# Cross-attention with two softmaxes per head: the first four query chunks, the K and V projections, the output matmuls and the V copies are put in another order

## The chip, the cores and the metric

The kernel runs on one core of one Trainium2 chip. The metric is the device time of one launch in microseconds (us), from the first to the last instruction and what lies around them; the median of three runs is compared. Of the core, six things matter: TensorE (PE in the profile), its weight load (PEld), VectorE (DVE), ScalarE (ACT), GpSimd (POOL) and the SyncE queue that issues every DMA (SP).

## The reference

A cross-attention layer with 20 heads of 32 channels: 2 batches of 2048 queries with 640 channels, and 154 context rows with 1024 channels for each batch. The context is split in two halves of 77 rows, each with its own K and V weights and its own softmax; the two results are added, projected, and added to the input.

```python
q = split_heads(x @ Wq.T)
k, v = split_heads(text @ Wk.T), split_heads(text @ Wv.T)            # rows 0..76
k_ip, v_ip = split_heads(ip @ Wk_ip.T), split_heads(ip @ Wv_ip.T)    # rows 77..153
out = merge_heads(attend(q, k, v)) + merge_heads(attend(q, k_ip, v_ip))
return out @ Wo.T + bo + x
# attend: softmax(q k^T / sqrt(32)) v, per head
```

Everything is float32, and so in the kernel.

## The kernel before

**Tiles.** Tokens are taken in 4 blocks `j` of 1024 (blocks 0 and 1 are batch 0, blocks 2 and 3 batch 1), each with two halves `h` of 512. The 640 channels are 5 chunks `c` of 128, that is of 4 heads. One pass of the main loop (line 323), called a step here, computes the attention of one chunk of one block: `m = 5 j + c`, 20 steps, and a 21st for what is left. A step goes through its 1024 queries in three groups `s` of 3, 3 and 2 tiles of 128 queries.

**What a step does.** `scores(m, s)` multiplies queries with keys on PE, four heads in four row strips of the array (line 190, 12 or 8 matmuls), and ACT copies the result from PSUM to `pb` (line 197). `maxima` finds the row maxima on DVE (204) and subtracts them on POOL (205); `exponential` is on ACT (211); `sums` adds the rows and takes the reciprocal on DVE (218, 220); `normalise` multiplies on POOL (225); `transpose` turns 32x32 squares on DVE (231) into `tT`. `attend(m - 1)`, one step later, multiplies with V in sixteen 32x32 tiles of the array (line 244, 80 matmuls), and ACT copies its result to `aT` (251). Beside that a step computes the queries of the step after it, two groups of 5 matmuls (`queries`, line 165, copied by ACT in 173).

**PSUM.** Scores and attention share one buffer of four banks (tag `sc`, one buffer). So a group of scores can start only when ACT has copied the group before, and `attend` likewise. The other four banks are the four buffers of tag `mm`: queries, K, V and output.

**K and V.** Steps 0 to 4 also project V of their own chunk (`project_v`, two groups of 8 matmuls, line 123, between the queries and `scores(m, 1)`) and K of the next chunk (`project_k`, two such groups before `attend`). ACT copies them (130, 135). V is turned on DVE (`square_v`, line 138) and then laid out four times over by 16 small DMAs (`spread_v`, line 147), for both batches at once. The 20 weight tiles pass through five slots in the not yet used `aT` of block 1; a new one is loaded when a projection has read its slot.

**Output.** `Out` v is one of 40 output tiles (a half of a block, 128 channels): 5 matmuls (line 275), then bias and input added on DVE (`store`, 286) and a DMA to memory (289). The input tile it adds (`res`) is fetched one output ahead (267). Step m works on outputs `2 (m - 5)` and the next: the first before `attend`, the second after it. So steps 0 to 4 have none, and 10 are left after step 19. In the first step of a block the last matmul of an output waits for the `attend` just ahead of it.

**Order.** The order of each engine's instructions is that of the program text (`manual_schedule`); the framework adds the semaphores. All DMAs go through SP in that order too, and SP waits at a DMA until its buffer is free. At the start SP issues: half the context, a weight tile, the other half, another weight tile, the first 128 columns of `Wq`, five pieces of x, the rest of the block's x, two weight tiles, the other columns of `Wq`, a weight tile. PE then projects K of chunk 0, computes the queries of step 0 and enters the loop.

Of the kernel before, what the change touches and what calls it, by code (L numbers as in the profile page):

```python
# [8 lines left out]
F32 = mybir.dt.float32  # L9
# [4 lines left out]
B, S, C, CC, LT = 2, 2048, 640, 1024, 154  # L14
H, D, TEXT = 20, 32, 77
# [4 lines left out]
def kernel(  # L20
# [23 lines left out]
    nc = tc.nc  # L44
    P = 128
    NC = C // P
    NCC = CC // P
    G = P // D
    TB = 512
    NH = 2  # L50
    BLK = NH * TB
    NT = BLK // P
    NBLK = B * S // BLK
# [3 lines left out]
    NK = (2 * L + D - 1) // D  # L57
    LP = NK * D
    SCALE = 1.0 / float(D) ** 0.5
    NM = NBLK * NC  # L60
    NV = NBLK * NH * NC
    LEAD = NC

    const = ctx.enter_context(tc.tile_pool(name="const", bufs=1))
    qpool = ctx.enter_context(tc.tile_pool(name="qpool", bufs=5))
    small = ctx.enter_context(tc.tile_pool(name="small", bufs=4))
    opool = ctx.enter_context(tc.tile_pool(name="opool", bufs=2))
    rpool = ctx.enter_context(tc.tile_pool(name="rpool", bufs=3))
    ps_s = ctx.enter_context(tc.tile_pool(name="ps_s", bufs=1, space=bass.MemoryType.PSUM))
    ps_m = ctx.enter_context(tc.tile_pool(name="ps_m", bufs=4, space=bass.MemoryType.PSUM))  # L70

    wq = const.tile([P, NC, C], F32, name="wq")
    bo_sb = const.tile([P, NC], F32, name="bo_sb")
    kT = const.tile([P, NC, B, 2, L], F32, name="kT")
    v4 = const.tile([P, NC, B, G, NK, D], F32, name="v4")
    xs = [const.tile([P, NC, BLK], F32, name=f"x_{n}") for n in range(2)]
    aTs = [const.tile([P, NC, BLK], F32, name=f"aT_{n}") for n in range(2)]
    tT = const.tile([P, NT, G, NK, D], F32, name="tT")
# [3 lines left out]
        nc.gpsimd.memset(t[:, :, :, 2 * L :], 0.0)  # L82

    vTs = [const.tile([P, B, LP], F32, name=f"vT_{n}") for n in range(2)]
    vSs = [const.tile([P, B, LP], F32, name=f"vS_{n}") for n in range(2)]
    for t in vTs:
        nc.gpsimd.memset(t[:, :, 2 * L :], 0.0)

# [8 lines left out]
    def block_of(m):  # L97

        j, c = divmod(m, NC)
        return j, c, j * BLK // S  # L100
# [7 lines left out]
    def load_w():  # L108
        n = len(loaded)
        if n < len(wlist):  # L110
            src, c = wlist[n]
            w = wslots[n % len(wslots)]
            nc.sync.dma_start(  # L113
                out=w, in_=src[:, ts(c, P)].rearrange("(k p) o -> p k o", p=P)
            )
            loaded.append(w)
# [12 lines left out]
    def project_k(c, t):  # L129
        nc.scalar.copy(kT[:, c, :, t, :], project_kv(4 * c + t, t, "pk"))  # L130

    def project_v(c):
        vT = vTs[c % 2]
        for t in range(2):
            nc.scalar.copy(vT[:, :, ds(t * L, L)], project_kv(4 * c + 2 + t, t, "pv"))

    def square_v(c):
        nc.vector.transpose(
            vSs[c % 2].rearrange("p b l -> p (b l)"),
            vTs[c % 2].rearrange("p b l -> p (b l)"),  # L140
        )

    def spread_v(c):

        for g in range(G):
            for r in range(G):
                nc.sync.dma_start(
                    out=v4[r * D : (r + 1) * D, c, :, g].rearrange("p b k d -> p b (k d)"),
                    in_=vSs[c % 2][g * D : (g + 1) * D],
                )  # L150


# [5 lines left out]

    qTs = {}

    def queries(m, h):
        j, c, _ = block_of(m)
        pq = ps_m.tile([P, TB], F32, tag="mm", name=f"pq_{m}_{h}")
        for k in range(NC):
            nc.tensor.matmul(  # L165
                pq,
                wq[:, k, ts(c, P)],
                xs[j % 2][:, k, ts(h, TB)],
                start=(k == 0),
                stop=(k == NC - 1),  # L170
            )
        qT = qpool.tile([P, TB], F32, tag="qT", name=f"qT_{m}_{h}")
        nc.scalar.copy(qT, pq)  # L173
        qTs[(m, h)] = qT


    def keys_of(s):
# [57 lines left out]

    def attend(m):

        j, c, b = block_of(m)
        pa = ps_s.tile([P, G, 512], F32, tag="sc", name=f"pa_{m}")
        for k in range(NK):  # L240
            for r in range(G):
                rows = slice(r * D, (r + 1) * D)
                for g in range(G):
                    nc.tensor.matmul(  # L244
                        pa[g * D : (g + 1) * D, r, : NT * D],
                        v4[rows, c, b, g, k, :],
                        tT[rows, :, g, k, :],
                        start=(k == 0),
                        stop=(k == NK - 1),
                    )  # L250
        nc.scalar.copy(  # L251
            aTs[j % 2][:, c, :].rearrange("p (n r s) -> p r n s", n=NT, r=G),
            pa[:, :, : NT * D].rearrange("p r (n s) -> p r n s", n=NT),
        )


    class Out:


        def __init__(self, v):  # L260
            self.v = v
            self.j, r = divmod(v, NH * NC)
            self.h, self.o = divmod(r, NC)
            self.tok = ds(self.j * BLK + self.h * TB, TB)

            self.res = rpool.tile([P, TB], F32, tag="res", name=f"res_{v}")
            nc.sync.dma_start(out=self.res, in_=xT[ts(self.o, P), self.tok])
            self.po = None
            self.k = 0

        def step(self, n):
            if self.po is None:
                self.po = ps_m.tile([P, TB], F32, tag="mm", name=f"po_{self.v}")
            for _ in range(n):
                nc.tensor.matmul(  # L275
                    self.po,
                    wo[:, self.k, ts(self.o, P)],
                    aTs[self.j % 2][:, self.k, ts(self.h, TB)],
                    start=(self.k == 0),
                    stop=(self.k == NC - 1),  # L280
                )
                self.k += 1

        def store(self):
            ot = opool.tile([P, TB], F32, tag="ot", name=f"ot_{self.v}")
# [2 lines left out]
            )  # L288
            nc.sync.dma_start(out=outT[ts(self.o, P), self.tok], in_=ot)

    outs = {}

    def out(v):

        for w in (v, v + 1):
            if 0 <= w < NV and w not in outs:
                outs[w] = Out(w)
        return outs.get(v)


    half = NCC // 2
    for k in (0, half):
        nc.sync.dma_start(  # L303
# [1 line left out]
            in_=ctxT[ds(k * P, half * P), :].rearrange("(k p) n -> p k n", p=P),  # L305
        )
        load_w()
    nc.sync.dma_start(out=wq[:, :, :P], in_=WqT[:, :P].rearrange("(k p) o -> p k o", p=P))
    for k in range(NC):
        nc.sync.dma_start(out=xs[0][:, k, :TB], in_=xT[ts(k, P), :TB])  # L310
    load_x(0, 1)
    load_w()
    load_w()
    nc.sync.dma_start(out=wq[:, :, P:], in_=WqT[:, P:].rearrange("(k p) o -> p k o", p=P))
    load_w()
    nc.sync.dma_start(out=bo_sb, in_=bo.rearrange("(c p) -> p c", p=P))
    for t in range(2):
        project_k(0, t)
    for h in range(NH):
        queries(0, h)  # L320

    late = None
    for m in range(NM + 1):
        j, c, _ = block_of(m)
        new = m < NM
        old = m >= 1
        kv = m < NC
        v = NH * (m - LEAD)
        if new:
            scores(m, 0)  # L330
        if old:
            normalise(m - 1, 2)
        if late:
            late.store()
            late = None
        if old:
            transpose(m - 1, 1)
            transpose(m - 1, 2)
        if new:
            maxima(m, 0)  # L340
        if new and m + 1 < NM:
            queries(m + 1, 0)
        if c == 2 and j + 1 < NBLK:
            for h in range(NH):
                load_x(j + 1, h)
        if kv:
            project_v(m)
        if m == NC - 1:
            nc.sync.dma_start(out=wo, in_=WoT.rearrange("(c p) o -> p c o", p=P))
        if new:  # L350
            scores(m, 1)
            maxima(m, 1)
            exponential(m, 0)
            sums(m, 0)
            normalise(m, 0)
        if kv:
            square_v(m)
            spread_v(m)
        if new and m + 1 < NM:
            queries(m + 1, 1)  # L360
        if new:
            scores(m, 2)
            maxima(m, 2)
            exponential(m, 1)
            sums(m, 1)
            normalise(m, 1)
        if m + 1 < NC:
            project_k(m + 1, 0)
        if m + 1 < NC:
            project_k(m + 1, 1)  # L370
        first = c == 0
        if v >= 0 and v < NV:
            if new:
                out(v).step(NC - 1 if first else NC)
                if not first:
                    out(v).store()
            else:
                for w in range(v, v + 3):
                    out(w).step(NC - 1)
        if old:  # L380
            attend(m - 1)
        if new:
            transpose(m, 0)
            exponential(m, 2)
            sums(m, 2)
        if v >= 0 and new:
            if first:
                out(v).step(1)
                out(v).store()
            out(v + 1).step(NC)  # L390
            late = out(v + 1)
    for w in range(NH * (NM - LEAD), NV):
        out(w).step(NC - out(w).k)
        out(w).store()


# [30 lines left out]
```

## Time and profile before

| | |
|---|---|
| three runs | 559.28, 560.77, 562.39 us (median 560.77) |
| the profiled execution | 561.68 us, of which the span of its instructions is 559.9 us |
| PE busy | 530.7 us, 95% of the span |
| DVE, POOL, ACT busy | 377.1, 351.5, 231.4 us |
| data moved | 50.57 MB, 90 GB/s in the mean |
| first matmul starts | 6.72 us |
| steps 0, 1, 2, 3, 4, 5 last | 22.3, 24.8, 24.8, 26.0, 23.5, 28.7 us |
| steps 6 to 9 last | 24.0 us each |
| from step 19's first scores to the last output matmul | 68.1 us |

A step's length is the time from its first matmul of `scores(m, 0)` to that of the next step. In the profile a line such as "L190 PE" is line 190 of the kernel before. A float32 matmul is recorded as two passes, so that 5 matmuls read "x10". The profile is of one execution; its views are the busy times, the groups of instructions, who waited for whom, the chain of work that ended last, the instructions in order of time, and the busy times of chosen windows with the clock that TensorE was granted.

### The profile page before, as it was taken

The numbers are of one execution on the slowest core, as the hardware profiler recorded it, in microseconds if no ns is written. First come the engines' busy times: TensorE is split into PE (matmuls) and PEld (weight loads), VectorE is DVE, ScalarE is ACT, GpSimd is POOL, SyncE is SP. The second block draws the span as 40 slices with busy tenths as digits, with TensorE's granted clock in tenths as the row PEclk, the third lists the DMA queues.
The fourth block names the chain that finished last, engine by engine and source line by source line (L and its number), as shares of the span: only waits on it lengthen the run. The fifth ranks groups of instructions, "written<-read, shape, count | busy, mean of one in ns | idle before, by whom it ended". The sixth has DMA issues, their size and how long they took to land.

```text
span 559.9 us, 12327 instructions
## 1 busy us (share of the span) xinstructions
PE 530.7 (95%) x5600; PEld 285.2 (51%) x5600; DVE 377.1 (67%) x285; ACT 231.4 (41%) x201; POOL 351.5 (63%) x129
## 2 busy tenths in 40 slices
PE   5899999989979999999999999999999999989997
PEld 5477666656534445454444544545445454444442
DVE  0138778665877878787777877778777787777211
ACT  1244555444543553535445354544525455351000
POOL 0047868584885858669594776959668695866000
PEclk9999999989989999999999999999999999989999
DMA  9943567523302162020101252111020211112252
GB/s 285 330 118 90 127 185 215 131 50 118 83 5 76 40 226 66 12 77 23 54 24 54 74 190 77 39 39 45 33 77 1 76 40 37 46 33 95 84 148 89
DMA packets 47765, 50.57 MB, mean 90 GB/s; under 512 B 3808, under 2 KB 31072, under 8 KB 47712
## 3 DMA queue, kind: packets, MB, share of 16 engines
q1 hardware_dynamic: 47712, 49.77, 30.1%
q8 instruction: 44, 0.72, 0.5%
q14 instruction: 9, 0.07, 0.0%
HBM read 36.00 MB, written 10.49 MB: 83 GB/s over the span
## 4 chain that ended last, share of the span: by engine, by line
PE 88%; DMA 3%; POOL 3%; ACT 3%; DVE 1%; issue 1%; SPq 1%
PE po L275 31%; PE pq L165 28%; PE pa L244 12%; PE sc L190 9%; PE pv L123 4%; DMA wq<-in_L_xattn_Wq_dram 3%; PE pk L123 3%; POOL pb L225 2%; ACT aT L251 1%; POOL pb L205 1%; ACT pb L197 1%; SPq L113 1%; DVE mx L204 1%; DVE tT L231 0%; SPq L303 0%
## 5 line engine op out<-in xcount | busy, mean ns | idle before, releaser
L205 POOL TENSOR_TENSOR pb<-pb,mx 128x1848 f32<-128x1848 f32 (+1 forms) x60 | 176.4, 2942 | 140.2 <-DVE mx L204 140.2
L225 POOL TENSOR_TENSOR pb<-pb,rden 128x1848 f32<-128x1848 f32 (+1 forms) x60 | 176.4, 2943 | 20.8 <-DVE rden L220 17.0
L275 PE MATMUL po<-aT,wo_ct 128*128 128x512 f32 x400 | 181.2, 604 | 4.5 <-ACT aT L251 4.5
L165 PE MATMUL pq<-x,wq 128*128 128x512 f32 x400 | 183.7, 607 | 1.4 <-DMA wq<-in_L_xattn_Wq_dram 1.4
L204 DVE TENSOR_REDUCE mx<-pb 128x24 f32<-128x1848 f32 (+1 forms) x60 | 109.8, 1833 | 75.2 <-ACT pb L197 75.2
L218 DVE TENSOR_REDUCE den<-pb 128x24 f32<-128x1848 f32 (+1 forms) x60 | 111.8, 1863 | 34.1 <-ACT pb L211 34.1
L231 DVE STREAM_TRANSPOSE tT<-pb 128x1920 f32<-128x1920 f32 (+1 forms) x60 | 115.2, 1939 | 21.6 <-PE pa L244 20.0
L275 PEld LDWEIGHTS po<-aT,wo_ct 128*128 128x128 f32 x400 | 73.9, 191 | 96.7 <-issue 89.7
L197 ACT COPY pb<-sc 128x1848 f32<-128x1848 f32 (+1 forms) x60 | 91.8, 1529 | 65.8 <-PE sc L190 64.4
L165 PEld LDWEIGHTS pq<-x,wq 128*128 128x128 f32 x400 | 73.3, 191 | 85.8 <-issue 83.6
L211 ACT ACTIVATE pb<-pb 128x1848 f32<-128x1848 f32 (+1 forms) x60 | 94.6, 1577 | 51.2 <-POOL pb L205 51.1
L244 PE MATMUL pa<-tT,v 32*32 32x256 f32 x3200 | 70.1, 392 | 4.3 <-ACT pb L197 3.3
L190 PEld LDWEIGHTS sc<-kT,qT 32*128 32x128 f32 x1280 | 45.1, 185 | 48.3 <-issue 37.2
L190 PE MATMUL sc<-kT,qT 32*128 32x154 f32 x1280 | 59.2, 310 | 8.4 <-ACT aT L251 4.4
L244 PEld LDWEIGHTS pa<-tT,v 32*32 32x32 f32 x3200 | 47.0, 103 | 29.5 <-ACT pb L211 8.3
L286 DVE SCALAR_TENSOR_TENSOR ot<-po,bo_sb,res 128x512 f32<-128x512 f32 x40 | 28.6, 715 | 46.6 <-PE po L275 43.4
L251 ACT COPY aT<-pa 128x1024 f32<-128x1024 f32 x20 | 20.2, 1012 | 80.9 <-PE pa L244 80.9
L173 ACT COPY qT<-pq 128x512 f32<-128x512 f32 x40 | 23.1, 578 | 62.9 <-PE pq L165 62.9
L123 PE MATMUL pk<-wo_ct,aT 128*128 128x154 f32 x160 | 25.3, 321 | 6.7 <-DMA aT<-in_L_xattn_Wk_dram 6.7
L123 PEld LDWEIGHTS pk<-wo_ct,aT 128*128 128x128 f32 x160 | 24.2, 210 | 7.3 <-issue 7.3
L123 PEld LDWEIGHTS pv<-wo_ct,aT 128*128 128x128 f32 x160 | 21.7, 188 | 2.4 <-issue 2.4
L123 PE MATMUL pv<-wo_ct,aT 128*128 128x154 f32 x160 | 21.9, 293 | 0.0
(11 smaller groups left out, 27.5 us busy)
## 6 DMA issues: line engine op xcount, KB each, us to landing
res<-in_x_dram SPq DMA_DIRECT2D x40, 256.0 KB, 3.4
out_dram<-ot SPq DMA_DIRECT2D x40, 256.0 KB, 2.4
x<-in_x_dram SPq DMA_DIRECT2D x7, 1280.0 KB, 9.4
v<-vS SPq DMA_DIRECT2D x80, 40.0 KB, 1.9
aT<-in_L_xattn_Wk_dram SPq DMA_DIRECT2D x5, 512.0 KB, 7.1
aT<-in_L_xattn_Wk_ip_dram SPq DMA_DIRECT2D x5, 512.0 KB, 4.6
aT<-in_L_xattn_Wv_dram SPq DMA_DIRECT2D x5, 512.0 KB, 5.7
aT<-in_L_xattn_Wv_ip_dram SPq DMA_DIRECT2D x5, 512.0 KB, 6.7
```

Source lines behind the costliest of these rows:

```text
L123: nc.tensor.matmul(out, loaded[n][:, k, :], cT[:, k, :, t, :], start=(k == 0), stop=(k == NCC - 1))
L165: nc.tensor.matmul(pq, wq[:, k, ts(c, P)], xs[j % 2][:, k, ts(h, TB)], start=(k == 0), stop=(k == NC - 1),)
L190: nc.tensor.matmul(ps[:, g, ts(t, 2 * L)], qTs[(m, h)][g * D : (g + 1) * D, ts(st, P)], kT[g * D : (g + 1) * D, c, b].rearrange("p t l -> ...
L197: nc.scalar.copy(keys_of(s), ps[:, :, : n * 2 * L].rearrange("p g (n l) -> p n g l", n=n))
L204: nc.vector.tensor_reduce(mx, rows_of(s), AX.X, ALU.max)
L205: nc.gpsimd.tensor_tensor(rows_of(s), rows_of(s), mx.unsqueeze(3).to_broadcast([P, n, 2, L]), ALU.subtract)
L211: nc.scalar.activation(e, e, AF.Exp, scale=SCALE)
L218: nc.vector.tensor_reduce(den, rows_of(s), AX.X, ALU.add)
L225: nc.gpsimd.tensor_tensor(rows_of(s), rows_of(s), rdens[s].unsqueeze(3).to_broadcast([P, n, 2, L]), ALU.mult)
L231: nc.vector.transpose(tT[:, first : first + n].rearrange("p n g k s -> p (n g k s)"), pbs[s].rearrange("p n g l -> p (n g l)"),)
L244: nc.tensor.matmul(pa[g * D : (g + 1) * D, r, : NT * D], v4[rows, c, b, g, k, :], tT[rows, :, g, k, :], start=(k == 0), stop=(k == NK - 1),)
L275: nc.tensor.matmul(self.po, wo[:, self.k, ts(self.o, P)], aTs[self.j % 2][:, self.k, ts(self.h, TB)], start=(self.k == 0), stop=(self.k == ...
```

## The change

The computation is the same. Six things are moved or resized.

1. At the start, the queries of the first half of block 0 are computed for **four** chunks together (`FIRST = 4`), slice by slice of the contracted dimension: after each slice of `Wq` (512 columns) and of x has come, four matmuls, one for each chunk, in four PSUM buffers. `Wq` and x are therefore loaded slice by slice ahead of everything else, and the query pool has 8 buffers in place of 5. Then come K of chunk 0 and the second half of step 0's queries. Steps 0 to 2 have one group of queries to compute in place of two.
2. `project_v` of the next chunk stands after `attend`, at the end of the step, in place of between the queries and `scores(m, 1)`; in step 0 V of chunk 0 also stands after `scores(0, 0)`. In steps 1 and 2 the first K group stands between `scores(m, 1)` and `scores(m, 2)`.
3. Outputs are a queue: `fill(n)` takes the next n output matmuls whose `aT` has been written, from up to three open outputs. It starts in step 4 (3 matmuls before `attend`, 4 after), does 5 and 5 in steps 5 to 18, and in step 19 4, 4, 3 and 4, the first two between its groups of scores. `flush` stores what has been finished, at two places of each step.
4. After the last `attend` the queue goes on; up to four outputs are open there.
5. `v4` holds V of one batch. Batch 0's copies are made as before, half as large; batch 1's are made by 16 DMAs after each `attend` of steps 6 to 10, over the chunk that this `attend` was the last to read. `vS` now keeps all chunks.
6. The input tiles `res` have 5 buffers in place of 3, and are fetched when an output is opened, for it and the next.

```diff
-    LEAD = NC
+    FIRST = 4
+    OPEN = 3
-    v4 = const.tile([P, NC, B, G, NK, D], F32, name="v4")
+    v4 = const.tile([P, NC, G, NK, D], F32, name="v4")
-    def spread_v(c):
+    def spread_v(c, b):
         for g in range(G):
             for r in range(G):
                 nc.sync.dma_start(
-                    out=v4[r * D : (r + 1) * D, c, :, g].rearrange("p b k d -> p b (k d)"),
-                    in_=vSs[c % 2][g * D : (g + 1) * D],
+                    out=v4[r * D : (r + 1) * D, c, g].rearrange("p k d -> p (k d)"),
+                    in_=vS[g * D : (g + 1) * D, c, b],
                 )
...
+    def fill(n, most=OPEN):
+        while n > 0:
+            o = next((o for o in opened if o.k < attended[o.j]), None)
+            if o is None:
+                v = len(finished) + len(opened)
+                if v == NV or len(opened) == most or attended[outs[v].j] == 0:
+                    return
+                for o in outs[v : v + 2]:
+                    o.fetch()
+                opened.append(outs[v])
+                continue
+            o.step()
+            n -= 1
+            if o.k == NC:
+                opened.remove(o)
+                finished.append(o)
+    def flush():
+        for o in finished[len(stored) :]:
+            o.store()
+            stored.append(o)
+    for k in range(NC):
+        nc.sync.dma_start(out=wq[:, k, : FIRST * P], in_=WqT[ts(k, P), : FIRST * P])
+        nc.sync.dma_start(out=xs[0][:, k, :TB], in_=xT[ts(k, P), :TB])
...
+    pqs = [ps_m.tile([P, TB], F32, tag="mm", name=f"pq_{m}_0") for m in range(FIRST)]
+    for k in range(NC):
+        for m in range(FIRST):
+            query_matmul(pqs[m], m, 0, k)
+    for m in range(FIRST):
+        keep_q(m, 0, pqs[m])
     for t in range(2):
         project_k(0, t)
-    for h in range(NH):
-        queries(0, h)
+    queries(0, 1)
     for m in range(NM + 1):
...
         if new:
             scores(m, 0)
         if old:
             normalise(m - 1, 2)
-        if late:
-            late.store()
+        flush()
...
-        if kv:
-            project_v(m)
+        if m == 0:
+            project_v(0)
+        elif m + 1 < FIRST:
+            queries(m + 1, 1)
+        if last:
+            fill(4)
         if new:
             scores(m, 1)
...
+        if 1 <= m < FIRST - 1:
+            project_k(m + 1, 0)
+        if last:
+            fill(4)
         if new:
             scores(m, 2)
...
+        if m >= NC - 1:
+            fill(3 if m < NC or last else 5)
+        flush()
         if old:
             attend(m - 1)
+            if not new:
+                fill(NC - 1, OPEN + 1)
+            attended[(m - 1) // NC] += 1
+            if (m - 1) // NC == NBLK // B - 1:
+                spread_v((m - 1) % NC, 1)
+        if m + 1 < NC:
+            project_v(m + 1)
...
         if new:
             transpose(m, 0)
             exponential(m, 2)
             sums(m, 2)
+            if m >= NC - 1:
+                fill(4 if m < NC or last else 5)
+    while len(finished) < NV:
+        fill(NC)
+        flush()
```

More of the change, by code (lines that the diff above doesn't have):

```diff
@@ L61 @@
     NV = NBLK * NH * NC
-    LEAD = NC
+    FIRST = 4
+    OPEN = 3
     const = ctx.enter_context(tc.tile_pool(name="const", bufs=1))
-    qpool = ctx.enter_context(tc.tile_pool(name="qpool", bufs=5))
+    qpool = ctx.enter_context(tc.tile_pool(name="qpool", bufs=2 * FIRST))
     small = ctx.enter_context(tc.tile_pool(name="small", bufs=4))
     opool = ctx.enter_context(tc.tile_pool(name="opool", bufs=2))
-    rpool = ctx.enter_context(tc.tile_pool(name="rpool", bufs=3))
+    rpool = ctx.enter_context(tc.tile_pool(name="rpool", bufs=5))
     ps_s = ctx.enter_context(tc.tile_pool(name="ps_s", bufs=1, space=bass.MemoryType.PSUM))
@@ L84 @@
     vTs = [const.tile([P, B, LP], F32, name=f"vT_{n}") for n in range(2)]
-    vSs = [const.tile([P, B, LP], F32, name=f"vS_{n}") for n in range(2)]
+    vS = const.tile([P, NC, B, LP], F32, name="vS")
     for t in vTs:
@@ L138, in square_v @@
         nc.vector.transpose(
-            vSs[c % 2].rearrange("p b l -> p (b l)"),
+            vS[:, c].rearrange("p b l -> p (b l)"),
             vTs[c % 2].rearrange("p b l -> p (b l)"),
         )
-    def spread_v(c):
+    def spread_v(c, b):
         for g in range(G):
@@ L159, with keep_q @@
     qTs = {}
[L161 to L171, printed above, removed]
+    def keep_q(m, h, pq):
         qT = qpool.tile([P, TB], F32, tag="qT", name=f"qT_{m}_{h}")
@@ L174, in queries, with query_matmul @@
         qTs[(m, h)] = qT
+    def query_matmul(pq, m, h, k):
+        j, c, _ = block_of(m)
+        nc.tensor.matmul(
+            pq,
+            wq[:, k, ts(c, P)],
+            xs[j % 2][:, k, ts(h, TB)],
+            start=(k == 0),
+            stop=(k == NC - 1),
+        )
+    def queries(m, h):
+        if m >= NM or (m, h) in qTs:
+            return
+        pq = ps_m.tile([P, TB], F32, tag="mm", name=f"pq_{m}_{h}")
+        for k in range(NC):
+            query_matmul(pq, m, h, k)
+        keep_q(m, h, pq)
     def keys_of(s):
@@ L236, in attend @@
     def attend(m):
-        j, c, b = block_of(m)
+        j, c, _ = block_of(m)
         pa = ps_s.tile([P, G, 512], F32, tag="sc", name=f"pa_{m}")
@@ L245, in attend @@
                         pa[g * D : (g + 1) * D, r, : NT * D],
-                        v4[rows, c, b, g, k, :],
+                        v4[rows, c, g, k, :],
                         tT[rows, :, g, k, :],
@@ L264, in __init__, with fetch, step @@
             self.tok = ds(self.j * BLK + self.h * TB, TB)
-            self.res = rpool.tile([P, TB], F32, tag="res", name=f"res_{v}")
-            nc.sync.dma_start(out=self.res, in_=xT[ts(self.o, P), self.tok])
-            self.po = None
+            self.res = self.po = None
             self.k = 0
-        def step(self, n):
+        def fetch(self):
+            if self.res is None:
+                self.res = rpool.tile([P, TB], F32, tag="res", name=f"res_{self.v}")
+                nc.sync.dma_start(out=self.res, in_=xT[ts(self.o, P), self.tok])
+        def step(self):
             if self.po is None:
                 self.po = ps_m.tile([P, TB], F32, tag="mm", name=f"po_{self.v}")
[L274 to L282, printed above, removed]
+            nc.tensor.matmul(
+                self.po,
+                wo[:, self.k, ts(self.o, P)],
+                aTs[self.j % 2][:, self.k, ts(self.h, TB)],
+                start=(self.k == 0),
+                stop=(self.k == NC - 1),
+            )
+            self.k += 1
         def store(self):
@@ L289, in store @@
             nc.sync.dma_start(out=outT[ts(self.o, P), self.tok], in_=ot)
[L291 to L298, printed above, removed]
+    outs = [Out(v) for v in range(NV)]
+    opened, finished = [], []
+    attended = [0] * NBLK
+    def fill(n, most=OPEN):
[4 more added lines that the diff above has]
+                if v == NV or len(opened) == most or attended[outs[v].j] == 0:
+                    return
+                for o in outs[v : v + 2]:
[7 more added lines that the diff above has]
+                finished.append(o)
+    stored = []
+    def flush():
[5 more added lines that the diff above has]
+        nc.sync.dma_start(out=xs[0][:, k, :TB], in_=xT[ts(k, P), :TB])
     half = NCC // 2
@@ L307 @@
         load_w()
-    nc.sync.dma_start(out=wq[:, :, :P], in_=WqT[:, :P].rearrange("(k p) o -> p k o", p=P))
-    for k in range(NC):
-        nc.sync.dma_start(out=xs[0][:, k, :TB], in_=xT[ts(k, P), :TB])
     load_x(0, 1)
@@ L313 @@
     load_w()
-    nc.sync.dma_start(out=wq[:, :, P:], in_=WqT[:, P:].rearrange("(k p) o -> p k o", p=P))
     load_w()
+    nc.sync.dma_start(
+        out=wq[:, :, FIRST * P :],
+        in_=WqT[:, FIRST * P :].rearrange("(k p) o -> p k o", p=P),
+    )
     nc.sync.dma_start(out=bo_sb, in_=bo.rearrange("(c p) -> p c", p=P))
+    pqs = [ps_m.tile([P, TB], F32, tag="mm", name=f"pq_{m}_0") for m in range(FIRST)]
+    for k in range(NC):
+        for m in range(FIRST):
+            query_matmul(pqs[m], m, 0, k)
+    for m in range(FIRST):
+        keep_q(m, 0, pqs[m])
     for t in range(2):
         project_k(0, t)
-    for h in range(NH):
-        queries(0, h)
-    late = None
+    queries(0, 1)
     for m in range(NM + 1):
@@ L326 @@
         old = m >= 1
-        kv = m < NC
-        v = NH * (m - LEAD)
+        last = m == NM - 1
         if new:
@@ L332 @@
             normalise(m - 1, 2)
-        if late:
-            late.store()
-            late = None
+        flush()
         if old:
@@ L340 @@
             maxima(m, 0)
-        if new and m + 1 < NM:
             queries(m + 1, 0)
@@ L345 @@
                 load_x(j + 1, h)
-        if kv:
-            project_v(m)
-        if m == NC - 1:
-            nc.sync.dma_start(out=wo, in_=WoT.rearrange("(c p) o -> p c o", p=P))
+        if m == 0:
[4 more added lines that the diff above has]
+            fill(4)
         if new:
@@ L355 @@
             normalise(m, 0)
-        if kv:
+        if m < NC:
             square_v(m)
-            spread_v(m)
-        if new and m + 1 < NM:
-            queries(m + 1, 1)
+            spread_v(m, 0)
+        queries(m + 1, 1)
+        if 1 <= m < FIRST - 1:
+            project_k(m + 1, 0)
+        if last:
+            fill(4)
         if new:
@@ L366 @@
             normalise(m, 1)
-        if m + 1 < NC:
+        if m == 0 or m == FIRST - 1:
             project_k(m + 1, 0)
@@ L370 @@
             project_k(m + 1, 1)
[L371 to L379, printed above, removed]
+        if m >= NC - 1:
+            fill(3 if m < NC or last else 5)
+        flush()
         if old:
             attend(m - 1)
+            if not new:
[5 more added lines that the diff above has]
+            project_v(m + 1)
+        if m + 1 == NC - 1:
+            nc.sync.dma_start(out=wo, in_=WoT.rearrange("(c p) o -> p c o", p=P))
         if new:
@@ L385 @@
             sums(m, 2)
[L386 to L394, printed above, removed]
+            if m >= NC - 1:
[3 more added lines that the diff above has]
+        flush()
 _TOKENS = ("x", "ctx_2048")
```

## The prediction

> **What bounds the kernel now.** First the page. PE is busy in 95% of the span, but its slices show where not: at the start, near slices 9 to 11, and at the end.
>
> ```profile
> PE 530.7 (95%) x5600; PEld 285.2 (51%) x5600; DVE 377.1 (67%) x285; ACT 231.4 (41%) x201; POOL 351.5 (63%) x129
> PE   5899999989979999999999999999999999989997
> ```
>
> Then the chain that ended last, in order of time. A steady step is PE alone:
>
> ```profile
> 196.84 1.00 PE sc L190 x24
> 197.84 4.49 PE pq L165 x10
> 202.33 1.00 PE sc L190 x24
> 203.33 4.49 PE pq L165 x10
> 207.81 0.74 PE sc L190 x16
> 208.55 4.49 PE po L275 x10
> 213.04 3.32 PE pa L244 x142
> 216.36 4.49 PE po L275 x10
> ```
>
> That sums to 24.0 us. Inside the tail's long run 34 passes take 14.79, so a query or output matmul (two passes) costs 0.86; five are 4.28, and 0.21 comes with each change from tiled to full-array work. A K or V group of 8 is 2.11. K and V steps (0 to 4) lack 8.98 of output work and have 8.65 of projections: PE work 23.7, 20.3 in step 0.
>
> The start, in the same chain, is DMA:
>
> ```profile
> 3.39 7.86 DMA wq<-in_L_xattn_Wq_dram
> 14.39 10.67 DMA wq<-in_L_xattn_Wq_dram
> ```
>
> Last the timeline at step 5, with the windows around it (PE busy is the first number after the width, then PEld, DVE, ACT, POOL; the third from the right is the granted clock):
>
> ```profile
> 158.12 1.75 ACT L211 ACTIVATE pb<-pb 128x1848 f32<-128x1848 f32 x1 [5.11 <-POOL pb L205]
> 160.24 1.19 ACT L197 COPY pb<-sc 128x1232 f32<-128x1232 f32 x1
> 161.48 4.75 PE L244 MATMUL pa<-tT,v 32*32 32x256 f32 x160 [1.98 <-ACT pb L197]
> ```
>
> ```profile
> 159.00:162.00 3.00, 1.02 (x35) 0.41 (x34) 2.08 (x1) 3.00 (x4) 2.33 (x1) 1.00 0.00 0
> 162.00:165.00 3.00, 3.00 (x120) 2.40 (x105) 2.99 (x3) 1.11 (x1) 2.54 (x1) 0.66 0.03 5
> ```
>
> Two things are seen. `attend` waits for the copy of the third score group, which stands on ACT behind the first exponential, which waits for POOL: where PE has less to do, a ring of ACT, DVE and POOL sets the pace. And after PE has idled about 2 us, the clock falls: this `attend` takes 4.75 in place of 3.3. Step 3 (idle 0.6 and 1.1) and step 19 (1.8 twice) lose clock too, about 1.7 us each.
>
> [...] for the start it records 1.00, yet the first K passes take 0.26 each (5 in the 1.28 us from 6.72) against 0.13 later, so I take it as cold. [...] before, 16 V copies hold SP for 11 us:
>
> ```profile
> 139.87 11.14 SPq L147 DMA_DIRECT2D v<-vS  x16
> ```
>
> **Part by part**, each against the same step of before.
>
> *Start, +9.7.* The loop began at 22.63. Before, 1128 KB (first context half and weight) had landed 5.98 us after the first issue; at 0.33 MB/us 3.5 of that is transfer and 2.5 fixed. The first slice pair is 512 KB: 0.74 + 2.5 + 1.6 = 4.8. Then 20 query matmuls, 17.1; a slice brings 3.4 us of work and 1.6 us of transfer, so DMA is covered. Context and two weights (4816 KB in all) are there at 18, the rest of x at 22, ahead of use. [...] K of chunk 0 4.2, the second query group 4.3, changes 0.2: 32.3. Nothing is thrown away, since 13.5 us of queries come out of steps 0 to 2.
>
> *Step 0, -2.0.* It lasted 22.26. Now three score groups 2.74, one query group 4.5, K and V of chunk 1 and V of chunk 0 12.9, a mode change 0.2: 20.3. No `attend` is in it.
>
> *Steps 1 and 2, +1.1.* PE work is 19.2, but the ring is longer. V's two groups follow `attend`, and ACT must copy both before it may start the third exponential. From one `attend` to the next: `attend` 3.32, two V groups 4.43, second V copy 0.29, exponential 1.24, sum and reciprocal 1.69, normalise 2.25, transpose 1.48, next maximum 2.06, subtraction 3.29, exponential 1.75, a K copy 0.29, score copy 1.19, and ten hand-overs of about 0.05: 23.7. PE idles 4 us before `attend`, so the clock falls: 1.7 more. Twice 25.4 against 49.7. Without the V groups (aT copy 1.0 in their place) the ring is 20, which PE's 24 hides; that is also the slack of a later step. V's weights come behind 11 us of V copies on SP, with 2 us to spare by my count.
>
> *Step 3, -2.0.* PE work and ring are both about 23.8, and the wait of `scores` for the aT copy (1.1) is covered by V: 24.0 against 26.04.
>
> *Step 4, +1.7.* Still behind the ring of step 3, PE waits 1.8 for `attend`; 1.1 for aT after it, as the queue's next matmul needs it; 7 output matmuls, 6.0, are new. 24.3, and half a clock fall, 0.9: 25.2 against 23.5.
>
> *Step 5, -3.5.* Its wait of 1.98 and clock fall are gone, the aT wait of 1.1 stays: 25.2 against 28.68.
>
> *Steps 6 to 10, 0.* SP has 16 more copies a step, from the end of `attend` on, with fetches, stores and the x loads behind them. A fetched input is needed some 20 us later, a stored tile's buffer half a step later: covered. Batch 1's copies are read five steps on.
>
> *Step 11, +5.9.* At its start three outputs are finished together (all three waited for the last `aT` of the block), and `opool` has two buffers. The third store waits on DVE until the first one's DMA has landed, and that stands on SP behind step 10's V copies. From the end of `attend`: 16 copies, a fetch 0.42, a store 0.35, landing 2.4. The copies took 0.68 each before; half as large they cost between 0.42 (a fetch's issue) and 0.68; I take 0.60: 9.6 + 3.2 = 12.8. Behind that store on DVE stand the transposes and the next maxima, for which POOL and the score copies wait. They begin at 13.5 where a steady step has 5.3: 8.2 late, less 4 of slack, 4.2. A clock fall: 1.7. At 0.42 the loss is 1.3, at 0.68 7.2 with its clock fall. Steps 6 and 16 also have three stores, but no V copies ahead of them: the third store waits 2 to 3 us, inside the slack.
>
> *Steps 12 to 18, -0.4.* Equal, but for a gap of 0.4 that I don't expect twice.
>
> *Step 19 and tail, -3.1.* It took 68.1 with 60 output matmuls; 53 are left: 45.3, scores 2.7, two `attend` 6.6, changes 1.3: 56.0. The score waits of 1.8 are filled, but the last `attend` stands ahead of all other outputs: its transposes end 25.6 us after the first scores (489.0 to 514.6 before), and the work between is 19.8 to 20.2, so PE waits 5.5. aT 1.1, a PSUM buffer 0.7, clock 1.7: 65.0. The close after the last matmul is the same.
>
> Sum: 9.7 - 2.0 + 1.1 - 2.0 + 1.7 - 3.5 + 5.9 - 0.4 - 3.1 = **+7.4**. On the profiled execution (561.68, span 559.9) that makes 569.1; the median of the runs is 0.9 below it: **568.2**.
>
> **Rivals.** *The V copies issue fast* (0.42): step 11 loses 1.3 and no clock. 568.2 - 4.6 = 563.6. For it: the size halves. Against: weight tiles of 512 KB issue in 0.4 too, so size seems not to set it.
>
> *The clock decides, and the time is not slower.* [...] 3.4 in steps 1 and 2, 0.9, 1.7 and 1.7 later are clock, 9.4 in all. If long gaps recover within themselves and the start is not cold, 558.8. The sign turns when less than 2.0 of the 9.4 is paid. For it: a window of 1.00 at the start, no fall at `attend` with gaps of 1.3. Against: each gap or pair of 1.7 us or more before led to a fall.
>
> *PE sets steps 1 and 2* (the third exponential isn't late). Twice 19.3 and no falls, and step 4 without its 1.8 and 0.9: 568.2 - 12.2 - 2.7 = 553.3. Against: the order of ACT's instructions puts both V copies ahead of it.
>
> *More is lost*: [...] 0.68 a copy, two falls in step 11, late weights: 574.
>
> **How the numbers follow.** Forecast 0.60 (564 to 572), fast copies 0.13, clock 0.10, PE pace 0.07, more 0.10. The range is 561.0 to 574.0: it leaves out PE pace and most of the clock case. A measurement here tells about 0.5% (2.8 us) from no change, that is 558.0 to 563.6. Faster 0.09 (PE pace, a little of the clock case), same 0.16 (the rest of it, half of the fast copies), slower 0.75.
>
> **What would show it.** Loop start at 32; `attend` in steps 1, 2 waiting 4 us for the score copy, steps of 25; step 11 near 30 with an output store waiting for an output DMA on DVE; the last `attend` waiting 5 us for a transpose; clock falls after each. Steps 1 and 2 at 20 us, or a step 11 of 24, would prove me wrong.

## The result, and the profile after

The changed kernel takes **567.5 us** (median of four runs, 567.1 to 568.7) against 560.25 (559.28 to 562.39) before: a ratio of 1.0128, 95% interval 1.0093 to 1.0162. Its profiled execution is 568.70 us, with a span of 566.9. The page's PE rows, then who PE waited for (us in total, times, longest):

```profile
PE 534.8 (94%) x5600; PEld 285.2 (50%) x5600; DVE 375.0 (66%) x285; ACT 232.0 (41%) x201; POOL 351.0 (62%) x129
PE   6999797999899999999999899999999999996997
PEclk9999988999999999999999899999999999999899
```

```profile
PE pa L253 <- ACT pb L206: 10.1, 4, 3.7
PE po L286 <- ACT aT L260: 5.8, 6, 1.2
PE pa L253 <- DVE tT L240: 5.0, 1, 5.0
```

PE does the same work with the same 5600 passes, but is busy 4.1 us longer than before: it runs slower in places. The holes that before had in slices 9 and 12 (steps 3 and 5; a slice here is 14.2 us) are gone, and a shallow one stands in slice 11 (step 4). New ones are in the fifth and seventh slice (steps 1 and 2), with the clock down in the sixth and seventh; both are down again in the 23rd (step 11). The hole near the end is deeper than before (6 in place of 8), with the clock down after it. Line 253 is `attend`, 206 the score copy, 240 the transpose, 148 the V copies, 297 and 300 the output store and its DMA.

The start, in the chain that ended last (start, us, what):

```profile
4.50 20.38 PE pq L169 x40
24.88 4.22 PE pk L124 x32
```

PE is not held by DMA once it has begun, but 40 passes take 20.38 us where at the full rate (0.43 each) they take 17.1. The same chain from step 1 to step 2:

```profile
53.87 1.24 ACT pb L220
...
57.01 2.26 POOL pb L234
59.30 1.51 DVE tT L240
60.81 1.97 DVE mx L213
62.84 3.29 POOL pb L214
...
68.08 1.10 ACT pb L206
69.22 5.60 PE pa L253 x157
74.82 4.70 PE pv L124 x32
```

This is a ring: the third exponential (53.87) is followed by sums, the last normalisation, its transpose, the next step's maximum and subtraction, the score copy, `attend`, the two V groups, and the next third exponential at 79.72. It closes in 25.85 us, which is step 1's length. `attend` takes 5.60 in it in place of 3.39, after a wait of 3.74. The window over it shows why (the granted clock is third from the right):

```profile
71.00:74.00 3.00, 3.00 (x112) 2.47 (x95) 3.00 (x2) 0.32 (x2) 3.00 (x2) 0.50 0.14 32
```

Step 11, in order of time:

```profile
293.74 10.60 SPq L148 DMA_DIRECT2D v<-vS  x16
...
308.55 0.75 DVE L297 SCALAR_TENSOR_TENSOR ot<-po,bo_sb,res 128x512 f32<-128x512 f32 x1 [8.89 <-DMA out_dram<-ot]
309.21 3.56 DVE L240 STREAM_TRANSPOSE tT<-pb 128x1920 f32<-128x1920 f32 x2
...
313.23 0.81 PE L199 MATMUL sc<-kT,qT 32*128 32x154 f32 x16 [2.14 <-ACT pb L206]
313.96 6.26 PE L286 MATMUL po<-aT,wo_ct 128*128 128x512 f32 x10
...
321.49 3.38 PE L253 MATMUL pa<-tT,v 32*32 32x256 f32 x160 [1.27 <-ACT pb L206]
```

The third output store stands on DVE for 8.89 us. It waits for the first one's DMA, which SP issues after the 16 V copies. Behind it on DVE are both transposes and the next maxima. PE then waits 2.14, does five output matmuls in 6.26 in place of 4.56, and waits 1.27 more: 5.1 of the 5.2 by which the step is longer.

### The profile page after: what moved, and what is told of

Same layout as the page of the kernel before. It is cut to its first block, busy times and chain, and to the rows that moved or that the text cites. A ratio compares the mean times of both kernels' runs of the same rounds, so it can differ in the third digit from the quotient of the medians.

```text
span 566.9 us, 12445 instructions
## 1 busy us (share of the span) xinstructions
PE 534.8 (94%) x5600; PEld 285.2 (50%) x5600; DVE 375.0 (66%) x285; ACT 232.0 (41%) x201; POOL 351.0 (62%) x129
## 4 chain that ended last, share of the span: by engine, by line
PE 80%; DVE 6%; POOL 5%; ACT 3%; issue 2%; DMA 1%; SPq 1%; POOLq 0%; DVEq 0%
PE pq L169 27%; PE po L286 27%; PE pa L253 12%; PE sc L199 7%; PE pv L124 4%; POOL pb L214 3%; DVE tT L240 3%; POOL pb L234 2%; PE pk L124 2%; DVE mx L213 2%; DVE den L227 1%; ACT aT L260 1%; ACT pb L220 1%; ACT pb L206 1%; DMA out_dram<-ot 1%
## 5 line engine op out<-in xcount | busy, mean ns | idle before, releaser
L234 POOL TENSOR_TENSOR pb<-pb,rden 128x1848 f32<-128x1848 f32 (+1 forms) x60 | 176.3, 2942 | 32.3 <-DVE rden L229 32.1
L286 PE MATMUL po<-aT,wo_ct 128*128 128x512 f32 x400 | 183.2, 607 | 5.9 <-ACT aT L260 5.8
L253 PE MATMUL pa<-tT,v 32*32 32x256 f32 x3200 | 73.8, 413 | 15.8 <-ACT pb L206 10.1
L253 PEld LDWEIGHTS pa<-tT,v 32*32 32x32 f32 x3200 | 49.9, 107 | 43.4 <-ACT pb L206 12.3
L124 PE MATMUL pk<-wo_ct,aT 128*128 128x154 f32 x160 | 22.9, 297 | 0.0
L124 PEld LDWEIGHTS pk<-wo_ct,aT 128*128 128x128 f32 x160 | 21.4, 188 | 1.4 <-issue 1.4
```

The costliest lines, as they stand in the source:

```text
L124: nc.tensor.matmul(out, loaded[n][:, k, :], cT[:, k, :, t, :], start=(k == 0), stop=(k == NCC - 1))
L234: nc.gpsimd.tensor_tensor(rows_of(s), rows_of(s), rdens[s].unsqueeze(3).to_broadcast([P, n, 2, L]), ALU.mult)
L253: nc.tensor.matmul(pa[g * D : (g + 1) * D, r, : NT * D], v4[rows, c, g, k, :], tT[rows, :, g, k, :], start=(k == 0), stop=(k == NK - 1),)
L286: nc.tensor.matmul(self.po, wo[:, self.k, ts(self.o, P)], aTs[self.j % 2][:, self.k, ts(self.h, TB)], start=(self.k == 0), stop=(self.k == ...
```

## The experiments

Each ratio is to the kernel before, timed beside the run; 567.5 stands at 1.0128. Timed there, the kernel before had medians of 560.75 to 561.12, 0.5 to 0.9 above its 560.25, so ratios are compared, not microseconds, where one or two matter. Step lengths here are taken between the first score copies of two steps, unless the text says otherwise.

**Step 11: three output buffers.**

```diff
-    opool = ctx.enter_context(tc.tile_pool(name="opool", bufs=2))
+    opool = ctx.enter_context(tc.tile_pool(name="opool", bufs=3))
```

> The changed kernel with three buffers for output tiles in place of two. If step 11 (29.3 us in the changed kernel) is long because its third store waits for the first one's DMA behind step 10's V copies, that store no longer waits: step 11 takes 24 to 25 us, VectorE has no wait for an output DMA there, no clock fall follows, and the time is 4.3 to 5.3 us less (562.2 to 563.2). Rival: three stores in a row ahead of the transposes are themselves too late, or the V copies slow something else in step 11; then it stays at 28 to 29 us and the time within 1 us of 567.5.

563.02 us, ratio 1.0034 (1.0020 to 1.0047). Step 11 lasts 24.00 in place of 29.25. In its timeline the 16 copies still take 11.04, but the three stores run together and nothing waits for them:

```profile
295.18 2.01 DVE L297 SCALAR_TENSOR_TENSOR ot<-po,bo_sb,res 128x512 f32<-128x512 f32 x3
```

The whole loss of step 11 came from the buffer that the third store lacked.

**Steps 1 to 3: free work ahead of `attend`.** Four matmuls whose result nothing reads, in steps 1 and 2:

```diff
+        if m in (1, 2):
+            pad = ps_m.tile([P, TB], F32, tag="mm", name=f"pad_{m}")
+            for k in range(4):
+                nc.tensor.matmul(pad, wq[:, k, :P], xs[0][:, k, :TB], start=(k == 0), stop=(k == 3))
         if old:
             attend(m - 1)
```

> The changed kernel with four more matmuls (their result is not used) ahead of attend in steps 1 and 2, where TensorE waits 3.7 us; they last 3.4 us. If the ring sets these steps and the idle time then costs clock, the added work is free and the clock stays up: steps 1 and 2 take 23.7 us each in place of 25.9 and 24.7, attend takes 3.4 in place of 5.6 and 4.7, and the time is 2 to 3.5 us less (564 to 565.5). Rival one: TensorE's work sets the steps; then each is 3.4 us longer and the time is 7 us more (574). Rival two: the long attend isn't a matter of the clock; then nothing changes (within 1 us).

564.06, ratio 1.0061 (1.0042 to 1.0079): more work, less time. Steps 1, 2, 3 are 23.36, 23.46, 23.85 against 25.85, 24.71, 24.91. The waits of `attend` for the score copy fall from 3.7 to 0.3 and 0.1 there, and `attend` is at its full rate in both steps, in step 1 for instance:

```profile
68.66 3.38 PE L253 MATMUL pa<-tT,v 32*32 32x256 f32 x160 [0.30 <-ACT pb L206]
```

So PE had at least 3.4 us to give in each of these steps; the ring with V's copies in it is 23.4, and of the 3.7 that stood above it in the two steps 3.6 was the slower `attend` (5.60 and 4.73, with a clock of 0.50 and 0.63 in the windows over them, against 3.38 and 3.39).

**Steps 1 to 3: V behind the third exponential.** The first attempt moved more than that:

```diff
-        if m + 1 < NC:
-            project_v(m + 1)
...
             exponential(m, 2)
             sums(m, 2)
+        if m + 1 < NC:
+            project_v(m + 1)
```

> The changed kernel with V of the next chunk written after the third exponential of the step in the program text. TensorE's order and every amount of work stay; only ScalarE now does the third exponential ahead of the two V copies. If the ring through these copies sets steps 1 and 2 (25.9 and 24.7 us), they fall to 20 to 21 us, attend waits less than 1 us there, its clock falls go, step 3 is 24.0 at most, and the time is 9 to 12 us less (556 to 558.5). Rival: GpSimd's 17.7 us and VectorE's 18 us of work a step, or weights that come late behind the V copies on the DMA queue, set the pace; then steps 1 and 2 stay at 23.5 or more and the time changes by less than 3 us.

589.9, ratio 1.0515 (1.0485 to 1.0545), but for another reason: the last `fill` of a step had come under the condition of the Wo load, so that it was never run. The outputs fell behind to the end and were then made from `aT` of later blocks. The total says nothing of the change. It showed something that I had not looked for: its steps from 5 on have 4.5 us of outputs less than 24.0, that is 19.5 of PE work, and still last about 22.2 each; its chain repeats every 22.2 us without PE. There is a second ring, of 22.2, without V. The edit alone, as meant:

> The changed kernel with only V of the next chunk moved behind the third exponential in the program text, and every output matmul where the changed kernel has it. The run before this one (where most output matmuls fell out of the steps) showed steps of 22.2 us without V copies in the ring: a second ring, GpSimd, VectorE and ScalarE through all four big GpSimd operations, closes behind the first. So the theory now says: the V copies cost the difference of the two rings. Steps 1, 2 and 3, 25.9, 24.7 and 24.9 us in the changed kernel, together 68 to 71 in place of 75.5, and the time 4.5 to 7.5 us less (560 to 563). The prediction's own ring of 20 us would give steps of 20 to 21 and 9 to 12 us less. Rival: late weights or nothing of the kind: no change.

561.7, ratio 1.0010 (0.9995 to 1.0024). Steps 1, 2, 3 are 23.39, 20.86 and 25.07, 6.1 less together. Over steps 1 and 2 its chain is again the second ring, 22.19 us from one third normalisation to the next, with PE nowhere in it. Taking V's copies from ahead of the exponential gives more than filling the wait does, as it shortens the ring itself.

**The start: a warm-up.** Seven matmuls of 256 columns on a constant ahead of the queries:

```diff
+    warm = const.tile([P, 256], F32, name="warm")
+    nc.gpsimd.memset(warm, 1.0)
...
+    pw = ps_s.tile([P, G, 512], F32, tag="sc", name="pw")
+    for k in range(7):
+        nc.tensor.matmul(pw[:, 0, :256], warm[:, :P], warm, start=(k == 0), stop=(k == 6))
```

> The changed kernel with seven matmuls on a constant tile ahead of the first query matmul, while TensorE waits for the first slice; their result is not used. In the changed kernel the 40 passes of the first queries take 20.4 us where warm ones take 17.1, and 8 of them fit into the first 5.5 us. If that is a cold clock, which the record shows as 1.00, activity from 1.5 us on uses up part of it: the passes take 17.1 to 18.8 us, and the time is 1.6 to 3.3 us less (564.2 to 565.9). Rival: the slices come too late one after another; then the passes still take 20 us and the time stays within 1 us of 567.5.

567.59, ratio 1.0118 (1.0079 to 1.0157): no gain. Its chain:

```profile
1.35 5.59 PE pw L356 x14
6.94 17.17 PE pq L171 x40
```

The 40 query passes now take 17.17, the full rate. The 14 warm-up passes wait for no DMA, yet took 0.40 each, where 0.21 is my estimate of the full rate for 256 columns, half of the 0.43 that the 512 columns of a query pass took: so the start is slow by itself, and not by slices that come late. But they held the first query back from 4.50 to 6.94, and the queries end at 24.1. With this start and no warm-up they end at 24.88 (the changed kernel), 24.32 (free work ahead of `attend`), 23.83 and 24.62 (V behind the third exponential, first attempt and as meant) and 23.99 (the start alone, the next run), so nothing was gained that stands out from that spread.

**The start alone, on the kernel before** (part 1, with 7 query buffers; V where it was; the loads' new order is left out here):

```diff
-    for h in range(NH):
-        queries(0, h)
+    pqs = [ps_m.tile([P, TB], F32, tag="mm", name=f"pq_{m}_0") for m in range(FIRST)]
+    for k in range(NC):
+        for m in range(FIRST):
+            query_matmul(pqs[m], m, 0, k)
...
+    queries(0, 1)
```

> The kernel before with the start alone: queries of four chunks slice by slice first, the loads in the changed order, 7 query buffers; V, output and copies as before. The loop begins at 33.3 in place of 22.6 us (10.7 later). If the second ring of 22.2 us sets the steps as soon as TensorE has less to do, steps 0, 1 and 2 (22.3, 24.8, 24.8) become about 17, 22.4 and 22.4, which gives back 10: the time is 0 to 3 us above the kernel before (560.5 to 563.5). Rival: TensorE's work sets the steps (17, 20.3, 20.3): 3 to 4 us below it (557). Second rival: the start is a plain loss, nothing comes back: 570.

560.44, ratio 0.9981 (0.9962 to 1.0001). The loop starts 9.8 later. Taken as in the table of the kernel before, from first score matmul to first score matmul, steps 0, 1 and 2 last 16.50, 22.88 and 22.20 in place of 22.3, 24.8 and 24.8, which gives 10.3 back. Steps 1 and 2 have 4.3 less work than before and get only 2.0 and 2.6 shorter, as the second ring takes over. Its chain shows it from one third normalisation to the next, 22.19 us, with PE nowhere in it:

```profile
54.81 2.26 POOL pb L232
57.09 1.51 DVE tT L238
...
60.65 3.30 POOL pb L212
...
65.74 2.09 DVE den L225
...
68.30 3.29 POOL pb L232
...
77.00 2.26 POOL pb L232
```

**The queue alone, on the kernel before** (parts 3, 4 and 6):

> The kernel before with the output queue alone (fill from step 4 on, in the last steps and the tail as changed, input tiles with 5 buffers); start, V and copies as before. The changed kernel's steps 4 and 5 last 49.2 us against 52.2 before, and from step 19 on 63.5 against 68.1. If these are the queue's doing and step 11 is long only through the V copies, this kernel takes 6 to 8.5 us less than the kernel before (552 to 554.5) and its step 11 is 24.0. Rival: the outputs moved ahead are only taken from a tail that then waits, and step 4 grows by what they need: within 3 us of the kernel before.

559.83, ratio 0.9969 (0.9953 to 0.9985), less than I expected. Step 5 is 25.18 and step 11 24.00, as expected without V copies in steps 6 to 10; but step 4 is 27.53, since there V of chunk 4 is projected in step 4, the Wo load waits for that, and the outputs wait for Wo:

```profile
126.45 4.23 PE pv L123 x32
...
130.69 6.93 DMA wo_ct<-in_L_xattn_Wo_dram
...
137.67 2.84 PE po L279 x6
```

The queue can start in step 4 without that wait because part 2 moves V, and with it Wo, into step 3.

**The tail: four matmuls of the queue ahead of the last `attend`** in place of behind it.

```diff
         if old:
+            if not new:
+                fill(NC - 1, OPEN + 1)
             attend(m - 1)
-            if not new:
-                fill(NC - 1, OPEN + 1)
```

> The changed kernel with the four output matmuls that follow the last attend put ahead of it (they use the four chunks attended before). If TensorE stands before the last attend only because the queue's matmuls are behind it, 3.4 of its 5.0 us of waiting are filled, the clock fall there is shorter or gone (up to 1.4), and the wait for aT after it comes back (1.1): 2.3 to 3.7 us less (563.8 to 565.2). Rival: the four matmuls only wait themselves, for a PSUM buffer or an input tile; then the time is within 1 us of 567.5.

564.03, ratio 1.0051 (1.0036 to 1.0067). The last `attend` waits 1.4 for the transpose in place of 5.0, and the waits for aT grow from 5.8 to 7.0.

**V after `attend` alone, on the kernel before** (part 2 without the moved K group; Wo still follows V of chunk 4):

```diff
-        if kv:
-            project_v(m)
+        if m == 0:
+            project_v(0)
...
             attend(m - 1)
+        if m + 1 < NC:
+            project_v(m + 1)
```

> Kernel before with V of the next chunk after attend alone, and Wo loaded after V of chunk 4 as there. If the move is harmful only because steps 1 and 2 lost query work to the start, it costs nothing here: PE has 23.7 of work in steps 1 to 3 against a ring of 23.4. Step 0 26.5 (it has V of chunk 1 too), steps 1 to 3 near 24.3, step 4 22.2 (bound by the ring, since it has no V), step 5 28.7 as before: 150 together as before, so 560.8, between 559 and 563. If the V copies ahead of the third exponential are harmful by themselves, steps 1 to 3 are 25 or more, with a wait of attend near 2 and a clock fall in each: 564 or more.

560.09, ratio 0.9977 (0.9961 to 0.9993). Steps 0 to 5 last 26.35, 23.86, 23.86, 24.45, 22.49, 26.52. The order that made steps 1 and 2 of the changed kernel 25.3 in the mean costs nothing where a step has its 23.8 of PE work. Step 4 has neither projections nor outputs, and there `attend` waits 4.16 and takes 5.60, as in the changed kernel's step 1.

**Two chunks at first in place of four**, with 5 query buffers, the rest of the change as it is:

```diff
-    FIRST = 4
+    FIRST = 2
...
-        if m == 0 or m == FIRST - 1:
+        if m == 0 or FIRST - 1 <= m < NC - 1:
             project_k(m + 1, 0)
```

> Changed kernel with two query chunks at first in place of four, so that steps 1 and 2 have both their query groups. Theory (the ring of 23.4 shows because the start took 4.3 of work out of steps 1 and 2): the loop starts two query groups, 8.6, earlier, near 24.7, and steps 1 and 2, now with 23.8 of work, get no longer than 24.9 each, without a wait of attend near 4: 567.5 - 8.6 - 0.8 = 558.1, between 556 and 560. If V after attend makes these steps long by itself (the copies delay the exponential whatever PE does, so that the added queries only push everything later), they are 28 and all of the 8.6 comes back: 566 to 568.

559.37, ratio 0.9965 (0.9947 to 0.9983). The loop starts at 25.4 (0.7 later than I said; the chain shows PE waiting for the second half of x, which lands at 20.85), and steps 1 and 2 are 23.86 each: two query groups of work more, and still 2.8 us shorter together. `attend` in step 1 starts at once and at full rate:

```profile
61.83 3.39 PE L253 MATMUL pa<-tT,v 32*32 32x256 f32 x160
```

Step 11 is 30.77 here. The same stall slows `attend` itself (4.78, after a wait of 2.97), where in the changed kernel the clock fell on matmuls ahead of a wait (five in 6.26, at 0.55).

**The gains together**, first with four chunks (three output buffers, matmuls ahead of the last `attend`, V behind the exponential), then with two chunks and V left where it was:

> Changed kernel with three edits that each gave something alone: three output buffers (-4.5), four output matmuls ahead of the last attend (-3.5), V behind the third exponential (-5.8), each measured against 567.5. They act in different steps (11; the tail; 1 to 4), so my theory says that they add: 553.7, between 552 and 556, step 11 at 24.0, steps 1 to 3 near 69.3 together, last attend waiting 1.4. The rival, that a part of each gain is the clock or slack that another edit also gives, says 556 to 560.

> Changed kernel with two query chunks at first, three output buffers and four output matmuls ahead of the last attend; V stays where the change put it. If the three act apart (start and steps 1 and 2; step 11; tail): 558.1 - 4.5 - 3.5 = 550.1, between 548 and 553, step 11 at 24.0, last attend waiting 1.4. If the start with two chunks gives nothing (steps 1 and 2 get longer by what the start gets shorter): 559.5.

551.3, ratio 0.9833 (0.9804 to 0.9863), and **549.06**, ratio 0.9792 (0.9764 to 0.9821). The single changes of ratio add: 1.0128 - 0.0094 - 0.0077 - 0.0118 = 0.9839 for the first, 1.0128 - 0.0163 - 0.0094 - 0.0077 = 0.9794 for the second. Both are faster than either kernel. What PE still waits for in the second (its mean granted clock is 1.00):

```profile
PE po L286 <- ACT aT L260: 6.9, 7, 1.2
PE pq L169 <- DMA x<-in_x_dram: 5.7, 2, 4.6
PE pa L253 <- DVE tT L240: 1.6, 1, 1.6
```

Part 5 alone (V of one batch) was not tried. What it cost here is seen from two sides: the queue without it has a step 11 of 24.00, and so has the whole change with a third buffer.

## Why the prediction was right, step by step

| step | predicted | measured |
|---|---|---|
| start | +9.7 | +10.7 (loop at 33.3) |
| step 0 | -2.0 | -2.0 |
| steps 1 and 2 | +1.1 | +0.9 (25.85, 24.71) |
| steps 3 and 4 | -2.0, +1.7 | -1.1, +0.6 |
| step 5 | -3.5 | -3.5 |
| steps 6 to 10 | 0 | +0.5 |
| step 11 | +5.9 | +5.2 |
| steps 12 to 18 | -0.4 | +0.3 |
| step 19 and tail | -3.1 | -4.6 |
| sum | +7.4 | +7.0 (spans: +7.0) |

The likeliest case came about, by its mechanisms. That the sum is off by only 0.4 is in part luck: the start, step 3, steps 6 to 10 and 12 to 18 cost 3.1 more than said, steps 1, 2, 4, 11 and the tail 3.5 less. And the end of the first queries alone differs by 0.8 us (23.83 to 24.62) between two runs that begin alike, the attempts with V behind the third exponential. One reading of the page was loose: before, the holes are in slices 9 and 12, that is in steps 3 and 5.

*Start.* The 32.3 is 1.7 more than the parts that rest on the profile (4.8, 17.1, 4.2, 4.3 and 0.2, together 30.6): an allowance for a slow start, whose size was my estimate and not shown. In the profiled execution the first seven passes, 6.0 us, ran at half rate (0.85 each, 0.43 after), and the 40 passes took 20.38 in place of 17.1: it cost 3.3. In the five kernels listed at the warm-up the 40 passes took 19.64 to 20.44, a cost of 2.5 to 3.3, so the allowance lay below all five. The first slice pair came at 4.5 rather than 4.8; the 0.33 MB/us in that sum is the second slice of the page of before, 330 GB/s.

*Steps 1 and 2.* The ring of 23.7 was sized well (23.4 with the wait filled). The sentence that without V's copies the ring is 20 is wrong: the start alone shows 22.2. I had followed one round through `attend` and not the one through POOL: two subtractions and three normalisations, with one exponential, sum, transpose and maximum between them. It moved steps 1 and 2 by nothing, but it means that steps in a row can be shortened by 1.8 us each and not by 4, and that the start could not have paid in full even without the V order: alone it takes 13.5 us of queries out of steps 0 to 2 and gets 10.3 back. What costs is two parts together: the start alone stands at 0.9981, V after `attend` alone at 0.9977, the whole change with two chunks at 0.9965, with four at 1.0128. No run has these two parts and nothing else; the last pair shows their effect within the whole change. The stall of step 11 is a loss of its own, 1.0128 to 1.0034.

*Steps 3 and 4* are -0.5 together against -0.3. In step 3 `attend` took 4.44 in place of 3.39, with a gap of 0.50 inside it for which the profile gives no reason. Before has the same in its step 3 (4.59, gap 0.62), and I had taken it as gone. In step 4 the wait was 1.39 in place of 1.8, and the clock fall of 0.9 did not come: `attend` took 3.38, with a clock of 1.00.

*Step 11.* The copies took 0.66 each and not 0.60 (before 0.70, with twice the bytes), so the next maxima came 8.4 later than in a steady step of before, where I had said 8.2 (and 9.0 later than in the run with three buffers). I took off 4 of slack and added 1.7 of clock. The fall came (a clock of 0.55 over 314 to 317) and cost 1.7, five output matmuls in 6.26 in place of 4.56, but ahead of a wait that it made shorter by as much: PE lost 2.14, 1.7 and 1.27, together 5.1, so 3.3 of the 8.4 was absorbed. The clock should not have been added; against it, the slack was a little smaller than 4 (3.3, or 3.8 against the run with three buffers, where the delay is 9.0 and the loss 5.2).

*Tail.* Ahead of the last `attend` PE waited 1.1 for aT and 5.0 for the transpose, together 6.1 (5.5 expected), and `attend` lost 1.4 (4.77 in place of 3.38, with a clock of 0.50 over 526 to 529; 1.7 expected). Behind it the 1.1 for aT and the 0.7 for a PSUM buffer did not come: the queue puts four matmuls of older chunks behind the last `attend`, which cover both, and I had charged them all the same.

*Rivals.* Fast V copies: refuted by 10.60 us for 16. Clock not paid: refuted. The 9.4 holds the allowance for the start. About 8.4 was paid: 3.3 by the slow first passes, 3.7 in steps 1 and 2 (by their lengths with free work in the gap), 1.4 at the last `attend`; step 4 had no fall, and that of step 11 cost nothing. PE pace in steps 1 and 2: refuted by the waits of 3.7. Even with V behind the exponential these steps take 22.1 in the mean, the second ring, and not the 19.3 of PE. More is lost: its 574 counted a larger loss at the start, again my estimate; the start cost 3.3 and a copy 0.66 where this case had set 0.68, but step 11 lost nothing to the clock, and the trace has no wait of PE for a weight tile.

## What to carry to other kernels

Work that is taken out of a step saves its time only down to the next ring of the other engines: follow each ring from an instruction to its own next round, and work out that length before you move work away (here 22.2 without and 23.4 with the V copies, against a step of 24). Moves that are free alone can cost together; try each alone and leave one out, and here half of a move (two chunks in place of four) was worth more than the whole. When outputs are finished in bursts, count the buffers of the store for the largest burst, not for the mean: the third one, behind a queue of small DMAs, stopped VectorE for 8.9 us.

## What the runs showed of the hardware that was not expected

At the start the profile gives a clock of 1.00, yet passes run at half rate for 6.0 us. In the windows of the changed kernel (PE busy first, with the number of passes; the clock is third from the right):

```profile
7.00:10.00 3.00, 3.00 (x5) 1.25 (x4) 0.00 (x0) 0.00 (x0) 0.00 (x0) 1.00 1.01 367
10.00:13.00 3.00, 3.00 (x7) 1.23 (x7) 0.00 (x0) 0.00 (x0) 0.00 (x0) 1.00 1.10 363
```

The slow start is read here from the spacing of the weight loads (0.85 until 10.5 us, 0.43 after), not from the clock's column. Its cost is not fixed: in the two runs with V behind the third exponential, which begin alike, the 40 query passes took 19.64 and 20.44 us.

Nor does a gap have a fixed price. Two gaps of 3.74 us in the changed kernel were followed by an `attend` of 5.60 and one of 4.73. Before, a gap of 1.98 led to one of 4.75, while with the start alone a gap of 2.11 was followed by one at full rate, 3.38. So the prediction's remark that every gap of 1.7 or more led to a fall holds for the kernel before and not for that run.

And a copy of 32 partitions from SBUF to SBUF held SP for 0.66 us with half the bytes (0.69 in the three-buffer run) and 0.70 with all of them: the time of SP here follows the count of such copies, hardly their size.
